# Packed expert weights, blocked activations and a re-cut last norm in a decoder layer with 64 experts

## The chip, the cores and the metric

The kernel runs on one core of one Trainium2 chip. The metric is the device time of one launch in microseconds (us); runs of a kernel are compared by their median. A profile is one execution of its own: its span is counted from the first instruction to the last, and its own time lies a little above its span.

A core has five engines with a program each: TensorE (PE, with its weight load shown apart as PEld), VectorE (DVE), ScalarE (ACT), GpSimd (POOL) and SyncE (SP). They meet through semaphores. SP, ACT and POOL issue the DMAs, which 16 DMA engines carry out.

## The reference, cut to what matters

One decoder layer in f32 on 32 batches of 256 tokens with 256 features. `_layernorm` comes after each part:

```python
x = _layernorm(x + attn(x))            # 16 heads, rotary positions
x = _layernorm(x + xattn(x, ctx))      # 120 context rows; two softmaxes per head,
                                       # weights a1 - lam * a2
x = _layernorm(x + ffn(x))
# ffn: 64 experts, the best 6 per token
scores = sigmoid(x @ router_weight.T)
top_idx = top_k(scores + expert_bias, 6)
probs = top_scores / (sum(top_scores) + 1e-20)
xs = rows of x, per expert, in 96 slots
y = gelu(xs @ w1[e]) @ w2[e]           # w1: 256x128, w2: 128x256
out[token] += y * probs
shared = gelu(x @ sw1.T) @ sw2.T       # 512 wide, for every token
```

## The kernel before, in words

**Order of the work.** Each engine is wrapped in a class `InOrder` (lines 163 to 188) that makes its instructions keep the order in which the program names them. All instructions are therefore recorded at line 172, and the profile tells them apart only by their tiles. What the kernel decides by hand is this one order per engine.

**Stage one** takes the 32 batches through both attentions and the routing. `Batch.steps` (lines 388 to 483) is a hand-written plan of entries (tick, part, function). A batch begins 16 ticks after the one before it, so several are under way together. In each tick the loop runs the part "pre", then the scores of up to two groups of heads with their row maxima (`maxima`, read by DVE into pad_mx) or their exponentials (`weights`, made by ACT into pt), then the parts "av" and "mm", and "post". Late in a batch's plan, at ticks 59 to 61, `xweigh` on DVE takes the products of the second attention (tr), a reciprocal and the coefficients into `parts`, and POOL subtracts the two into `at`. At ticks 73 to 81 `route` chooses the six experts on DVE (step 2 removes the maxima found so far, and counts the tokens of each expert). `dispatch` then sends each token's row with an indirect DMA from POOL into its slot of `slots`: x, its 64 weights and its number, 1284 bytes. `store` (line 964) writes three things through SP: the transposed activations `x2T_d`, and the starting values of the two arrays `acc`: x in the first, zero in the second.

**The shared feed-forward** is a generator `shared` (lines 204 to 275), cut into pieces and threaded between other work. It goes by 16 blocks of 512 tokens. For each block `load` brings x2T from `x2T_d` through SP, two pieces on PE make h (ACT's gelu turns it into gT), and two pieces one block later make the output, which ACT copies to `y`. Each piece is followed by its ACT operation only when the next piece begins. Two banks of PSUM hold h.

**Stage two** (lines 1010 to 1230) runs the experts by pairs, 32 of them, one pair per turn of its loop ("slot"). A pair goes through four steps, one slot apart: `turn` (PE transposes the expert's rows xs; DVE copies them to xsT), `up` (PE), `gelu` (ACT, hT), `down` (PE), and `scatter`: DVE weighs the two results into `ye` (six buffers), and POOL issues two indirect DMAs that add the 96 rows of each expert into `acc[0]` and `acc[1]`. There are 64 such scatters. Experts are loaded by groups of four: `rows_of` brings xs, `expert_weights` w1t and w2t, with three groups loaded ahead; from then on a group is fetched whenever two pairs are through `down`, 13 fetches, of which the first (at 1703 us) lies before the first scatter and 12 lie among the scatters. All the loads are issued by SP. In two of three slots one piece of the shared feed-forward is run too; from the slot END on, two in each slot.

**The last norm** begins at END. A class `Last` has one object per block of 512 tokens: `fetch` (SP loads both sums from acc), `add` (POOL adds them), `stats` (DVE adds y, takes mean and variance in mv), `scale` (POOL makes rs = variance + eps, rstd = rs to the power of -1/2, and off = -mean * rstd), and `put` (ACT scales and shifts into `o`, SP issues the store). A loop runs add of one block, stats and scale of the one before, and put of the one before that. The tile pool `four` with 10 buffers of 4 KB per partition serves w1t, w2t, the sums a and the outputs o.

Of the kernel before, what the change touches and what calls it, by code (L numbers as in the profile page):

```python
# [36 lines left out]
def tile_decoder_layer(  # L37
# [15 lines left out]
    lams: list,  # L53
    router_wT: bass.AP,
    expert_b: bass.AP,
    w1: bass.AP,
    w2: bass.AP,
    sw1T: bass.AP,
    sw2T: bass.AP,
    out: bass.AP,  # L60
# [3 lines left out]
    S = condT.shape[2]  # L64
    NI = T // P
    NT = B * T
    assert T == 2 * P and S <= P

    const = ctx.enter_context(tc.tile_pool(name="const", bufs=1))
# [3 lines left out]

    slots = dram.tile([NE * CAP, XPW], F32, name="slots")
    acc = [dram.tile([NT + CAP, D], F32, name=f"acc{n}") for n in range(2)]
    x2T_d = dram.tile([D, NT], F32, name="x2T_d")

    ident = const.tile([P, P], F32, name="ident")
    make_identity(nc, ident)
# [117 lines left out]
        return trp.tile([P, 512], F32, tag="tr", name="tr")  # L197


    TB = min(512, NT)  # L200
    NQ = TB // P
    NBLK = NT // TB
    ys, whole = {}, set()
# [1 line left out]
    def shared(ypool):  # L205


        def load(k):
            t = ffn.tile([P, D // P, TB], F32, tag="x2T", name="x2T", bufs=3)
            sp.dma_start(  # L210
                out=t,
                in_=x2T_d[:, k * TB : (k + 1) * TB].rearrange("(c p) t -> p c t", p=P),
            )
            return t

        def gelu(hp, gT):

            act.activation(
                gT.rearrange("p f (q t) -> p f t q", q=NQ),
                hp[:, :, :TB].rearrange("p f (t q) -> p f t q", q=NQ),  # L220
                AF.Gelu_apprx_tanh,
            )

        def keep(k, q2, ps):
            if q2 == 0:
                ys[k] = ypool().tile([P, NQ, D], F32, tag="y", name="y")
            act.copy(ys[k][:, 2 * q2 : 2 * q2 + 2, :], ps)
            if 2 * q2 + 2 == NQ:
                whole.add(k)

        before = None
        loaded = {k: load(k) for k in range(2)}
        gTs = {}
        for k in range(NBLK + 1):
            for f2 in range(2):
                if k == NBLK:
                    continue
                if f2 == 0 and k + 2 < NBLK:
                    loaded[k + 2] = load(k + 2)
                if before:  # L240
                    before()
                hp = scp.tile([P, 2, 512], F32, tag="sc", name="h")
                for f in range(2):
                    f0 = (2 * f2 + f) * P
                    for c in range(D // P):
                        pe.matmul(
                            hp[:, f, :TB],
                            lhsT=w_s1[:, c, f0 : f0 + P],
                            rhs=loaded[k][:, c, :],
                            start=(c == 0),  # L250
                            stop=(c == D // P - 1),
                        )
                gT = gTs[k, f2] = ffn.tile([P, 2, TB], F32, tag="gT", name="gT", bufs=4)
                before = lambda hp=hp, gT=gT: gelu(hp, gT)
                yield
            for q2 in range(NQ // 2):
                if k == 0:
                    continue
                if before:
                    before()  # L260
                ps = bank().rearrange("p (q d) -> p q d", q=2)
                for q in range(2):
                    for f in range(SF // P):
                        pe.matmul(
                            ps[:, q, :],
                            lhsT=gTs[k - 1, f // 2][
                                :, f % 2, (2 * q2 + q) * P : (2 * q2 + q + 1) * P
                            ],
                            rhs=w_s2[:, f, :],
                            start=(f == 0),  # L270
                            stop=(f == SF // P - 1),
                        )
                before = lambda k=k, q2=q2, ps=ps: keep(k - 1, q2, ps)
                yield
        before()
        yield
# [5 lines left out]
    with ExitStack() as one:  # L282
# [101 lines left out]
        class Batch:  # L384
# [13 lines left out]
            def steps(self):  # L398
# [64 lines left out]
                    (60, "mm", self.xback, 0),  # L463
                    (61, "pre", self.xweigh, 0),
                    (61, "mm", self.xback, 1),
                    (62, "pre", self.xweigh, 1),
                    (64, "mm", self.transpose, "bT", lambda: self.at),
                    (65, "pre", self.moved, "bT"),
                    (65, "mm", self.project, "bT", "o", w_xout),
# [7 lines left out]
                    (73, "pre", self.sigmoid),  # L477
                    (73, "post", self.route, 0),
                    (75, "post", self.route, 1),
                    (77, "post", self.route, 2),  # L480
                    (79, "post", self.route, 3),
                    (80, "post", self.route, 4),
                    (81, "mm", self.places),
# [480 lines left out]
            def store(self):  # L964

                cols = slice(self.b * T, (self.b + 1) * T)
                sp.dma_start(
                    out=x2T_d[:, cols].rearrange("(c p) t -> p c t", p=P), in_=self.t["x2T"]
                )
                sp.dma_start(  # L970
                    out=acc[0][cols, :].rearrange("(i p) d -> p i d", p=P),
                    in_=self.xpt[:, :, :D],
                )
                sp.dma_start(
                    out=acc[1][cols, :].rearrange("(i p) d -> p i d", p=P),
                    in_=zero[:, :D].unsqueeze(1).to_broadcast([P, NI, D]),
                )
# [33 lines left out]
    with ExitStack() as two:  # L1011
# [1 line left out]
        four = two.enter_context(tc.tile_pool(name="four", bufs=10))  # L1013
        wk = two.enter_context(tc.tile_pool(name="wk2", bufs=2))
        small = two.enter_context(tc.tile_pool(name="small2", bufs=3))
        ypool = two.enter_context(tc.tile_pool(name="ypool", bufs=NBLK))
        ypools.append(ypool)
        EG = 4
        START = 7
# [20 lines left out]
            dve.tensor_add(idx, token, empty)  # L1040
            return idx

        def expert_weights(eg):
            es = slice(eg * EG, (eg + 1) * EG)
            w1t = four.tile([P, EG, D // P, F], F32, tag="four", name="w1t")
            sp.dma_start(out=w1t, in_=w1[es].rearrange("e (c p) f -> p e c f", p=P))
            w2t = four.tile([P, EG, D], F32, tag="four", name="w2t")
            sp.dma_start(out=w2t, in_=w2[es].rearrange("e p d -> p e d"))
            return w1t, w2t

        class Pair:


            def __init__(self, n):
                self.es = (2 * n, 2 * n + 1)

            def turn(self):
# [13 lines left out]
            def up(self):  # L1071
                self.ps = bank()[:, : 2 * CAP].rearrange("p (e t) -> p e t", e=2)
                for k, e in enumerate(self.es):
                    for c in range(D // P):
                        pe.matmul(
                            self.ps[:, k, :],
                            lhsT=weights_of[e // EG][0][:, e % EG, c, :],
                            rhs=self.xsT[:, k, c, :],
                            start=(c == 0),
                            stop=(c == D // P - 1),  # L1080
                        )
# [5 lines left out]
            def down(self):  # L1087
                self.ps = bank()[:CAP].rearrange("p (e d) -> p e d", e=2)
                for k, e in enumerate(self.es):
                    pe.matmul(  # L1090
                        self.ps[:, k, :],
                        lhsT=self.hT[:, k, :],
                        rhs=weights_of[e // EG][1][:, e % EG, :],
                        start=True,
                        stop=True,
                    )
# [24 lines left out]
        class Last:  # L1121
# [16 lines left out]
            def stats(self):  # L1138
# [4 lines left out]
                for q in range(NQ):  # L1143
                    dve.bn_stats(st[:, q, :], y[:, q, :])
                    dve.bn_aggr(mv[:, q, :], st[:, q, :])

            def scale(self):
                rs = small.tile([P, NQ], F32, tag="rs", name="rs")
                pool.tensor_scalar(rs, self.mv[:, :, 1], LN_EPS, None, ALU.add)
                self.rstd = small.tile([P, NQ], F32, tag="rstd", name="rstd")  # L1150
                pool.tensor_tensor(self.rstd, rs, mhalf[:, :NQ], ALU.pow)
                self.off = small.tile([P, NQ], F32, tag="off", name="off")
                pool.tensor_tensor(self.off, self.mv[:, :, 0], self.rstd, ALU.mult)
                pool.tensor_scalar(self.off, self.off, -1.0, None, ALU.mult)

            def put(self):
                o = four.tile([P, NQ, D], F32, tag="four", name="o")
                for q in range(NQ):
# [4 lines left out]
                        scale=self.rstd[:, q : q + 1],  # L1163
                        bias=self.off[:, q : q + 1],
                    )
                sp.dma_start(
                    out=flat[self.rows, :].rearrange("(p q) d -> p q d", q=NQ), in_=o
                )

# [1 line left out]
        pairs = [Pair(n) for n in range(NP)]  # L1171
        xs_of, idx_of, weights_of = {}, {}, {}
        last = [Last(k) for k in range(NBLK)]
        END = START + NP + 3
        slot = steps = 0
        more = True

        def pieces_on(n):
            nonlocal more
            for _ in range(n):  # L1180
                if more:
                    more = next(pieces, "end") != "end"

        def fetch_for(eg):
            if eg < NE // EG:
                xs_of[eg] = rows_of(eg)
                weights_of[eg] = expert_weights(eg)

        while more or steps < NBLK + 3:
            n = slot - START  # L1190
# [6 lines left out]
                pairs[n - 3].scatter()  # L1197
            if slot == 1:
                for eg in range(3):
                    weights_of[eg] = expert_weights(eg)  # L1200
            if slot == START - 2:
                for eg in range(3):
                    xs_of[eg] = rows_of(eg)
# [7 lines left out]
                pieces_on(2)  # L1211
            if slot >= END and (steps == 0 or steps > NBLK or steps - 1 in whole):
                for part, behind in (
                    (Last.add, 0),
                    (Last.stats, 1),
                    (Last.scale, 1),
                    (Last.put, 2),
                ):
                    if part is Last.add:
                        for k in range(0 if steps == 0 else steps + 2, min(steps + 3, NBLK)):  # L1220
# [15 lines left out]
def _rotary(seq):  # L1236
# [3 lines left out]
    ).astype(np.float32)  # L1240
    angles = (np.arange(seq, dtype=np.float32)[:, None] * freqs[None, :]).astype(np.float64)
    return [np.repeat(f(angles).astype(np.float32), 2, axis=1) for f in (np.cos, np.sin)]


# [45 lines left out]
```

## Time and profile before

| | us |
|---|---|
| median of 3 runs | 1999.38 (1996.08 to 2007.22) |
| the profiled execution's own time | 2002.98 |
| its span | 2001.2 |
| PE busy | 1903.4 (95%) |
| DVE, POOL, ACT busy | 1244.2, 1185.4, 1013.0 |
| PE's mean granted clock | 0.978 of full |

Attention and routing fill the span to about 1650 us, then come the last dispatches (the last is done at about 1700), the experts (to about 1900) and the last norm. In the table of the profile by stage each row gives the stretch, its length, busy time and number of instructions of PE, PEld, DVE, ACT and POOL, the granted clock, the mean busy share of the DMA engines and what they moved. A line of the waits is: the waiting engine and the tile it goes on to write, what it waited for, the total in us, how often, the longest. A line of the timeline is: start, duration, engine, operation with output and inputs and their shapes, how many in a row, and in brackets the idle time before it with what ended it. A DMA line gives the size of each DMA in KB and the median time from issue to landing.

### The profile page before, as it was taken

What the parts mean: (1) busy time and instruction counts of PE and PEld (TensorE: products, weight loads), DVE (VectorE), ACT (ScalarE), POOL (GpSimd) and SP (SyncE); (2) the same over time, 40 slices, a digit from 0 to 9 for tenths busy, and PEclk for the clock granted to TensorE, in tenths of its full rate; (3) what the DMA queues carried; (4) which work ended last, traced back from release to release, by engine and by line L of the source; (5) the groups of instructions that cost most, each with busy time, mean ns of one, the idle gap of its engine ahead of it and who ended that gap; (6) DMA issues with size and microseconds to landing.
All of it is one profiled execution on the core that took longest, in us unless ns stands there. A gap on an engine that the chain in (4) does not pass through costs nothing.

```text
span 2001.2 us, 43322 instructions
## 1 busy us (share of the span) xinstructions
PE 1903.4 (95%) x17800; PEld 1298.4 (65%) x17800; DVE 1244.2 (62%) x2750; ACT 1013.0 (51%) x1445; POOL 1185.4 (59%) x1191
## 2 busy tenths in 40 slices
PE   6999999999999999999999999999999988998977
PEld 3566666666666666666666666666666655766745
DVE  3366777777777777777777777777776643232155
ACT  1445555555555555555555555555555442321356
POOL 6233466666666666666666666666664455244687
PEclk8899999999999999999999999999999979998989
DMA  9100121111111111111111111111100023787495
GB/s 250 47 14 9 34 74 59 49 43 35 36 34 32 34 34 35 33 34 32 32 37 31 32 31 33 32 31 31 32 20 20 18 64 101 193 205 178 65 328 210
DMA packets 131813, 132.06 MB, mean 66 GB/s; under 512 B 32763, under 2 KB 118996, under 8 KB 131616
## 3 DMA queue, kind: packets, MB, share of 16 engines
q1 hardware_dynamic: 103408, 115.22, 18.9%
q0 software_dynamic: 25600, 13.02, 3.9%
q8 instruction: 140, 2.29, 0.5%
q10 hardware_dynamic: 2608, 1.07, 0.3%
q14 instruction: 57, 0.47, 0.1%
HBM read 74.62 MB, written 111.04 MB: 93 GB/s over the span
## 4 chain that ended last, share of the span: by engine, by line
PE 80%; DVE 8%; DMA 6%; POOL 3%; issue 2%; ACT 1%; DVEq 0%; POOLq 0%; SPq 0%; ACTq 0%
PE tr L172 39%; PE sc L172 26%; PE av L172 12%; DMA acc<-ye,idx 5%; PE h L172 3%; DVE pad_mx L172 2%; DVE parts L172 1%; POOL slots L172 1%; ACT pt L172 1%; DVE rd L172 1%; DVE rest L172 1%; DVE count L172 1%; DVE ye L172 1%; DVE sel L172 0%; DMA a<-acc 0%
## 5 line engine op out<-in xcount | busy, mean ns | idle before, releaser
L172 DVE TENSOR_REDUCE pad_mx<-sc 128x4 f32<-128x1024 f32 (+1 forms) x512 | 608.3, 1189 | 373.7 <-PE sc L172 367.3
L172 ACT ACTIVATE pt<-sc 128x1024 f32<-128x1024 f32 (+1 forms) x512 | 523.6, 1025 | 399.6 <-PE sc L172 399.3
L172 PE MATMUL sc<-qT,kT 32*128 32x256 f32 (+1 forms) x4096 | 574.0, 405 | 12.3 <-ACT pt L172 7.8
L172 PE MATMUL sc<-kT,qT 32*128 32x256 f32 (+1 forms) x4096 | 562.1, 394 | 10.5 <-ACT pt L172 5.3
L172 POOL DMA_INDIRECT slots<-xpt,slot x384 | 388.9, 1013 | 95.5 <-issue 91.0
L172 PEld LDWEIGHTS sc<-qT,kT 32*128 32x128 f32 (+1 forms) x4096 | 340.2, 183 | 127.7 <-issue 66.0
L172 PEld LDWEIGHTS sc<-kT,qT 32*128 32x128 f32 x4096 | 347.5, 184 | 93.2 <-DVE pad_mx L172 24.5
L172 POOL TENSOR_TENSOR qT<-qT,mT 128x512 f32<-128x512 f32 x128 | 163.5, 1296 | 144.9 <-ACT mT L172 144.9
L172 PE MATMUL tr<-w_qkv,xT 128*128 128x256 f32 (+1 forms) x512 | 193.0, 511 | 8.6 <-DMA xT<-in_xT 8.6
L172 POOL TENSOR_SCALAR rs<-mv 128x2 f32<-128x2 f32 (+1 forms) x80 | 31.0, 388 | 241.9 <-DVE mv L172 240.6
L172 POOL DMA_INDIRECT acc<-ye,idx x64 | 90.1, 1408 | 108.5 <-DVE ye L172 54.4
L172 ACT COPY ot<-av 128x512 f32<-128x512 f32 x192 | 112.3, 585 | 78.5 <-PE av L172 78.4
L172 PEld LDWEIGHTS tr<-w_qkv,xT 128*128 128x128 f32 x512 | 90.6, 191 | 77.7 <-issue 72.4
L172 PE MATMUL av<-pt,pad_v 128*32 128x256 f32 x2048 | 125.3, 385 | 10.2 <-DVE parts L172 10.2
L172 PE MATMUL h<-x2T,w_s 128*128 128x512 f32 x256 | 116.1, 603 | 13.7 <-DMA a<-acc 12.0
L172 PE MATMUL av<-pt,pad_xv 120*32 120x256 f32 x2048 | 126.8, 388 | 0.1
L172 POOL TENSOR_TENSOR rc<-qkb,cosr 128x512 f32<-128x512 f32 x64 | 82.5, 1289 | 71.7 <-DVE qkb L172 66.6
L172 PE MATMUL tr<-w_s,gT 128*128 128x256 f32 x512 | 117.2, 387 | 1.1 <-DVE ye L172 1.1
L172 ACT COPY kT<-tr 128x512 f32<-128x512 f32 (+1 forms) x128 | 70.3, 574 | 89.3 <-PE tr L172 89.3
L172 PEld LDWEIGHTS tr<-w_s,gT 128*128 128x128 f32 x512 | 99.5, 195 | 19.3 <-issue 3.8
L172 POOL TENSOR_TENSOR at<-parts 128x256 f32<-128x256 f32 x64 | 46.4, 725 | 107.3 <-DVE parts L172 107.3
L172 POOL TENSOR_TENSOR pad_qk<-rc,qkb 128x256 f32<-128x256 f32 x128 | 104.9, 841 | 5.0
(141 smaller groups left out, 2844.3 us busy)
## 6 DMA issues: line engine op xcount, KB each, us to landing
a<-acc SPq DMA_DIRECT2D x32, 512.0 KB, 5.6
xT<-in_xT SPq DMA_DIRECT2D x32, 256.0 KB, 6.5
xt<-in_x SPq DMA_DIRECT2D x32, 256.0 KB, 2.8
x2T_d<-T SPq DMA_DIRECT2D x32, 256.0 KB, 2.2
acc<-xpt SPq DMA_DIRECT2D x32, 256.0 KB, 2.7
acc<-zero SPq DMA_DIRECT2D x32, 256.0 KB, 3.0
x2T<-x2T_d SPq DMA_DIRECT2D x16, 512.0 KB, 7.8
w1t<-in_w SPq DMA_DIRECT2D x16, 512.0 KB, 6.8
```

Of the source, the lines that this page charges most:

```text
L172: ins = f(*args, **kwargs)
```

## The change

It has five parts.

1. The experts' weights are packed on the host, one array per pair of experts: for each of 128 partitions, and each expert of the pair, the two halves of w1 and then w2, 512 values. A pair's load is one DMA of 128 rows of 4 KB, 32 loads in all. Before, w1t came in rows of 512 B and w2t in rows of 1 KB, 16 loads each, for groups of four experts. The bytes are the same, and so are PE's instructions.
2. `x2T_d` is laid out by blocks of 512 tokens, so that a block's load has 128 rows of 4 KB where it had 256 of 2 KB. The stores keep pieces of 1 KB. The loads have four buffers and run three blocks ahead, issued in the second h piece of a block.
3. `xweigh` of the second half moves from the start of tick 62 to the end of tick 61, and step 2 of `route` from the end of tick 77 to the start of tick 78. Tick 61 of one batch is tick 77 of the one before it, so the two swap places on DVE.
4. In the last norm DVE makes rs and off; POOL keeps only the power. `put`'s store is issued by ACT. Per step the order is offset, put, add, stats, scale.
5. The pool of y has 14 buffers, was 16; END is one slot later; the slot in between (its n is 35, and 35 % 3 is 2) has neither a pair nor a piece.

The diff, cut:

```diff
-    x2T_d = dram.tile([D, NT], F32, name="x2T_d")
+    x2T_d = dram.tile([NT // TB, P, D // P, TB], F32, name="x2T_d")
...
-            t = ffn.tile([P, D // P, TB], F32, tag="x2T", name="x2T", bufs=3)
-            sp.dma_start(
-                out=t,
-                in_=x2T_d[:, k * TB : (k + 1) * TB].rearrange("(c p) t -> p c t", p=P),
-            )
+            t = ffn.tile([P, D // P, TB], F32, tag="x2T", name="x2T", bufs=4)
+            sp.dma_start(out=t, in_=x2T_d[k])
...
-        loaded = {k: load(k) for k in range(2)}
+        loaded = {k: load(k) for k in range(3)}
...
-                if f2 == 0 and k + 2 < NBLK:
-                    loaded[k + 2] = load(k + 2)
+                if f2 == 1 and k + 3 < NBLK:
+                    loaded[k + 3] = load(k + 3)
...
-                    (62, "pre", self.xweigh, 1),
+                    (61, "post", self.xweigh, 1),
...
-                    (77, "post", self.route, 2),
+                    (78, "pre", self.route, 2),
...
-                sp.dma_start(
-                    out=x2T_d[:, cols].rearrange("(c p) t -> p c t", p=P), in_=self.t["x2T"]
-                )
+                k, t0 = divmod(self.b * T, TB)
+                sp.dma_start(out=x2T_d[k, :, :, t0 : t0 + T], in_=self.t["x2T"])
...
-        ypool = two.enter_context(tc.tile_pool(name="ypool", bufs=NBLK))
+        ypool = two.enter_context(tc.tile_pool(name="ypool", bufs=NBLK - 2))
...
-            w1t = four.tile([P, EG, D // P, F], F32, tag="four", name="w1t")
-            sp.dma_start(out=w1t, in_=w1[es].rearrange("e (c p) f -> p e c f", p=P))
-            w2t = four.tile([P, EG, D], F32, tag="four", name="w2t")
-            sp.dma_start(out=w2t, in_=w2[es].rearrange("e p d -> p e d"))
-            return w1t, w2t
+            wt = four.tile([P, 2, D // P * F + D], F32, tag="four", name="wt")
+            sp.dma_start(out=wt, in_=w12[n])
+            return wt
...
+                self.rs = small.tile([P, NQ], F32, tag="rs", name="rs")
+                dve.tensor_scalar(self.rs, mv[:, :, 1], LN_EPS, None, ALU.add)
...
-                pool.tensor_scalar(rs, self.mv[:, :, 1], LN_EPS, None, ALU.add)
...
-                pool.tensor_tensor(self.off, self.mv[:, :, 0], self.rstd, ALU.mult)
-                pool.tensor_scalar(self.off, self.off, -1.0, None, ALU.mult)
+                dve.scalar_tensor_tensor(
+                    self.off, self.mv[:, :, 0], -1.0, self.rstd, ALU.mult, ALU.mult
+                )
...
-                sp.dma_start(
+                act.dma_start(
                     out=flat[self.rows, :].rearrange("(p q) d -> p q d", q=NQ), in_=o
                 )
...
-        END = START + NP + 3
+        END = START + NP + 4
...
+        def weights_for(eg):
+            for n in range(eg * EG // 2, (eg + 1) * EG // 2):
+                weights_of[n] = expert_weights(n)
...
                 for part, behind in (
+                    (Last.offset, 2),
+                    (Last.put, 2),
                     (Last.add, 0),
                     (Last.stats, 1),
                     (Last.scale, 1),
-                    (Last.put, 2),
```

More of the change, by code (lines that the diff above doesn't have):

```diff
@@ L55, in tile_decoder_layer @@
     expert_b: bass.AP,
-    w1: bass.AP,
-    w2: bass.AP,
+    w12: bass.AP,
     sw1T: bass.AP,
@@ L66, in tile_decoder_layer @@
     NT = B * T
+    TB = min(512, NT)
     assert T == 2 * P and S <= P
@@ L197, in bank @@
         return trp.tile([P, 512], F32, tag="tr", name="tr")
-    TB = min(512, NT)
     NQ = TB // P
@@ L1041, in tokens_of, with expert_weights @@
             return idx
-        def expert_weights(eg):
-            es = slice(eg * EG, (eg + 1) * EG)
-            w1t = four.tile([P, EG, D // P, F], F32, tag="four", name="w1t")
-            sp.dma_start(out=w1t, in_=w1[es].rearrange("e (c p) f -> p e c f", p=P))
-            w2t = four.tile([P, EG, D], F32, tag="four", name="w2t")
-            sp.dma_start(out=w2t, in_=w2[es].rearrange("e p d -> p e d"))
-            return w1t, w2t
+        def expert_weights(n):
+            wt = four.tile([P, 2, D // P * F + D], F32, tag="four", name="wt")
+            sp.dma_start(out=wt, in_=w12[n])
+            return wt
         class Pair:
             def __init__(self, n):
+                self.n = n
                 self.es = (2 * n, 2 * n + 1)
@@ L1076, in up @@
                             self.ps[:, k, :],
-                            lhsT=weights_of[e // EG][0][:, e % EG, c, :],
+                            lhsT=weights_of[self.n][:, k, c * F : (c + 1) * F],
                             rhs=self.xsT[:, k, c, :],
@@ L1092, in down @@
                         lhsT=self.hT[:, k, :],
-                        rhs=weights_of[e // EG][1][:, e % EG, :],
+                        rhs=weights_of[self.n][:, k, D // P * F :],
                         start=True,
@@ L1145, in stats, with offset @@
                     dve.bn_aggr(mv[:, q, :], st[:, q, :])
+                self.rs = small.tile([P, NQ], F32, tag="rs", name="rs")
+                dve.tensor_scalar(self.rs, mv[:, :, 1], LN_EPS, None, ALU.add)
             def scale(self):
-                rs = small.tile([P, NQ], F32, tag="rs", name="rs")
-                pool.tensor_scalar(rs, self.mv[:, :, 1], LN_EPS, None, ALU.add)
                 self.rstd = small.tile([P, NQ], F32, tag="rstd", name="rstd")
-                pool.tensor_tensor(self.rstd, rs, mhalf[:, :NQ], ALU.pow)
+                pool.tensor_tensor(self.rstd, self.rs, mhalf[:, :NQ], ALU.pow)
+            def offset(self):
                 self.off = small.tile([P, NQ], F32, tag="off", name="off")
-                pool.tensor_tensor(self.off, self.mv[:, :, 0], self.rstd, ALU.mult)
-                pool.tensor_scalar(self.off, self.off, -1.0, None, ALU.mult)
+                dve.scalar_tensor_tensor(
+                    self.off, self.mv[:, :, 0], -1.0, self.rstd, ALU.mult, ALU.mult
+                )
             def put(self):
@@ L1186, in fetch_for @@
                 xs_of[eg] = rows_of(eg)
-                weights_of[eg] = expert_weights(eg)
+                weights_for(eg)
         while more or steps < NBLK + 3:
@@ L1199, in tile_decoder_layer @@
                 for eg in range(3):
-                    weights_of[eg] = expert_weights(eg)
+                    weights_for(eg)
             if slot == START - 2:
@@ L1242, in _rotary, with _pairs_of_experts @@
     return [np.repeat(f(angles).astype(np.float32), 2, axis=1) for f in (np.cos, np.sin)]
+def _pairs_of_experts(w1, w2):
+    up = w1.reshape(NE, D // P, P, F).transpose(0, 2, 1, 3).reshape(NE, P, D // P * F)
+    both = np.concatenate([up, w2], axis=2)
+    return both.reshape(NE // 2, 2, P, -1).transpose(0, 2, 1, 3)
 def kernel(**inputs):
@@ L1270 @@
         "expert_b": a["L0_ffn_expert_bias"],
-        "w1": a["L0_ffn_w1"],
-        "w2": a["L0_ffn_w2"],
+        "w12": _pairs_of_experts(a["L0_ffn_w1"], a["L0_ffn_w2"]),
         "sw1T": a["L0_ffn_sw1"].T,
```

## The prediction, made before the result was known

> **What bounds the kernel now.** I read the page first, then the windows by stage, the waits, the DMA view of the expert stage, and the timeline where a wait ends.
>
> ```profile
> PE 1903.4 (95%) x17800; PEld 1298.4 (65%) x17800; DVE 1244.2 (62%) x2750; ACT 1013.0 (51%) x1445; POOL 1185.4 (59%) x1191
> ...
> PE 80%; DVE 8%; DMA 6%; POOL 3%; issue 2%; ACT 1%; DVEq 0%; POOLq 0%; SPq 0%; ACTq 0%
> ```
>
> The matmul engine carries the chain. The windows (us, then busy and count for PE, PEld, DVE, ACT, POOL, then clock, DMA share, GB/s) show where it does not:
>
> ```profile
> 160.00:1500.00 1340.00, 1329.42 (x14158) 907.18 (x14158) 964.40 (x2069) 763.10 (x1098) 844.51 (x858) 1.00 0.12 35
> ...
> 1750.00:1800.00 50.00, 47.14 (x256) 35.41 (x254) 15.67 (x45) 12.36 (x19) 20.76 (x15) 1.00 0.89 213
> 1800.00:1850.00 50.00, 41.99 (x192) 31.18 (x193) 13.49 (x41) 8.13 (x14) 23.26 (x18) 0.90 0.77 177
> ...
> 1900.00:1950.00 50.00, 38.01 (x122) 23.57 (x121) 26.69 (x73) 26.37 (x37) 40.81 (x38) 0.86 0.92 333
> ```
>
> The attention loop leaves PE 10.6 us idle in 1340. The expert stage has DMA at 0.77 to 0.89, and PE begins to stall in it. The waits (us, times, longest) say for what:
>
> ```profile
> DVE ye L172 <- DMA acc<-ye,idx: 63.2, 16, 8.1
> ```
>
> The 64 scatters add rows into two arrays. Their landing frees the six ye buffers, and PE waits behind DVE. The DMA view while weights load (1720 to 1780), and its scatter row after the loads end (1850 to 1900; last column us to landing):
>
> ```profile
> w1t<-in_w SPq DMA_DIRECT2D x7, 512.0 KB, 7.2
> w2t<-in_w SPq DMA_DIRECT2D x7, 512.0 KB, 6.8
> xs<-slots SPq DMA_DIRECT2D x7, 481.5 KB, 4.6
> x2T<-x2T_d SPq DMA_DIRECT2D x2, 512.0 KB, 10.1
> acc<-ye,idx POOLq DMA_INDIRECT x19, 6.5
> ```
> ```profile
> acc<-ye,idx POOLq DMA_INDIRECT x23, 3.3
> ```
>
> A load burst costs a scatter 3.2 us. From the timeline: scatter 1 is issued at 1719.60, the last at 1897.38, landing about 1902.4; four scatters (one burst) take 11.4 to 14 us while loads run, 8.2 us after. The excess is about 3.75 us per burst (12 fetches of a group lie among the scatters), 45 us. PE alone needs 4.37 us per pair, 140 us for 32 pairs, so some 28 us at most could be won there before PE binds. The timeline of PE's stall at its longest, and of the stage of the last norm (start, us, engine, operation, then idle time before it and who ended it):
>
> ```profile
> 1834.37 2.02 PE L172 MATMUL tr<-w2t,hT 128*96 128x256 f32 x4 [4.89 <-DVE ye L172]
> ...
> 1912.17 1.22 POOL L172 TENSOR_SCALAR rs<-mv 128x4 f32<-128x4 f32 x1
> ...
> 1924.52 9.42 PE L172 MATMUL h<-x2T,w_s 128*128 128x512 f32 x16 [11.99 <-DMA a<-acc]
> ...
> 1989.59 7.97 ACT L172 ACTIVATE o<-y,off,rstd 128x256 f32<-128x256 f32 x16
> ```
>
> PE stops at 1912.5 and resumes at 1924.52, because a gelu on ACT stands behind two puts that wait for the sum of the scattered rows. The time of the end follows the last scatter's landing one to one (PE resumes 22 us after it), then PE runs to 1989, and ACT makes four puts.
>
> **Packed weights.** 32 loads of 512 KB stay 32 loads of 512 KB; the rows change from 512 B and 1 KB to 4 KB. In the trace's packets a 512 B row takes 34 to 37 ns, a 1 KB row 47 to 51, a 1284 B row of xs 79 to 82, a 2 KB row 84 to 105 and a 4 KB row (a, out) 159 to 180. Per DMA engine (of 16) a burst is now xs 24 x 0.080 = 1.9 us, w1t 64 x 0.035 = 2.2, w2t 32 x 0.049 = 1.6: 5.7 us. After it is 1.9 + 2 x 8 x 0.170 = 4.6: 1.1 us less. Times 12 is 13 us of DMA time, not on any path unless a scatter waits for it. One end is therefore -12 us. For the other end I ask what stands ahead of a scatter. The rows that went ahead of the delayed ones count 78 to 91 per engine, or about 55 KB: the 24 of xs and most of the 64 of w1t (up to 4.1 us), while w2t comes behind. With 4 KB rows there are 24 + 16, and the nearest row is scatter 63, which met one a load in 4 KB rows: 7 of the 8 rows per engine went first (1.6 us). So all that has arrived goes first: 1.9 + 2.7 = 4.6, +0.5 us for the first scatter of a burst; the second one, which stood behind the whole 5.7, gets 1.1 us back. The two scatters feed two arrays whose chains run side by side, each waiting for its own last landing, with POOL issuing both in order; the later one sets the pace. Between +0.6 and -1.0 per burst I take the middle, -0.2: 12 x -0.2 = **-2 us**; ends -12 and +7.
>
> [...]
>
> **Activations by blocks.** 16 loads of 256 x 2 KB become 128 x 4 KB: 16 x 0.09 = 1.4 us per engine now, 8 x 0.17 = 1.4 after: nothing. Three loads go ahead instead of two, half a step earlier, in a fourth buffer; PE waits for no x2T, so nothing is won. On SP the first three and then a fourth load come before the last batches' stores; those stores (0.36 us issue) wait behind them for at most one issue each. In 4 to 5 bursts an x2T load meets a scatter, 1.4 us in which 2 KB rows could be overtaken and 4 KB rows, by scatter 63, cannot. I take 0; up to +7 (5 x 1.4).
>
> **Weighing before the choice.** A pure swap on DVE: six operations of 1107.82 to 1109.56 (1.74 us) go ahead of the top-6 selection (1106.69 to 1107.8, 1.1 us). The parts come 1.1 us sooner, POOL's at too, and "PE av <- DVE parts" (10.2 us in 27 batches, 0.35 in the batch I followed) may go. But the next thing PE waits for is the reduction behind both, 1109.56 to 1110.71 (PEld sc waits 0.41 for it), and DVE has no gap from 1099.66: it ends where it did. So the stall moves to the scores 1.9 us later. I take 0; ends -9.5 (all of it) and +2 (the dispatch, whose slots come later by 1.7 us once).
>
> **Last norm.** On POOL, rs (1.22 to 1.27 us beside a DVE add; 0.23 in the tail where DVE is idle), and two small ones (0.20 + 0.25) leave for DVE as two operations of 128x4; DVE's 0.1 to 0.2 us rows of that size price them at 0.3 together. For the first block 1.25 + 0.45 - 0.3 is about 1.25 us, in line with put, gelu and PE's resumption: **-1.25 us**. In the later blocks POOL's cycle of 5.39 us hides beneath PE's 6.9 us per slot, and stays hidden; the new one (DVE statistics 3.45, rs, pow 1.04 on POOL, off, semaphores: about 5.1) hides as well. DVE's off now waits for POOL's pow with the next block's statistics behind it; cover 6.9 - 5.1 = 1.8 us.
>
> The 16 out stores move from SP to ACT. Issues on ACT in the trace's start take 0.34 to 0.49 us, and ACT first waits for its own writes. In the stream this hides (ACT is busy 31.28 of 52 us), but behind it stand gelus for which PE's h bank waits: put 2.08 + two gelus 3.7 + 0.6 = 6.4 of 6.9 us. In the tail it doesn't: after the last copy ACT makes four puts in 7.97 us without a gap, and three issues now lie between them, 3 x (0.4 + 0.15) = **+1.65 us**; ends 0 and +3. SP's fetches no longer queue behind a store: nothing, since DMA (0.92) and PE bind there. The y buffers, two fewer, and END, one slot later in which no piece falls, change no order on PE: nothing.
>
> Sum: 0 - 2 + 0 - 1.25 + 1.65 = -1.6. Against the profiled execution's own 2002.98 (span 2001.2) that is 2001.4; the median of the runs is 3.6 lower, 1999.38, so I say 1998 for the likeliest case.
>
> **Rivals.** (1) The bursts' work is the price: the later scatter binds, and each burst gives 1.0 us back: -12 - 1.25 + 1.65 = -11.6, 1988. For it: DMA is near full (0.89), so less work must show somewhere; against: landings wait for what is ahead, not for the mean. A further end, no scatter delay at all, would be -28, 1971. (2) Slower: long rows shut the scatters out. The first scatter of a burst binds, +0.5 in 7 bursts and 0.5 + 1.4 in 5 with an x2T load: 3.5 + 9.5 = +13, 2012; it is slower than a measurement can tell from about +0.85 us a burst. For it: scatter 63; against: w2t's rows no longer follow. (3) The swap doesn't do what it says, or all: 0 or -9.5.
>
> **Numbers.** Likeliest case (within some 8 us of 1998) 0.44; rival 1 0.28, with its far end 0.04 of that; rival 2 0.24; rival 3's gain 0.04. The range takes in rivals 1 and 2, 1984 to 2014. A measurement tells about 0.5%, 10 us: faster 0.30, same 0.45, slower 0.25.
>
> **What would show it.** Right: packets of wt near 170 ns; scatter landing near 6.5 us still while loads run; last scatter issued near 1895; first put 1.25 us sooner after the first sum; ACT's tail near 9.5 us instead of 7.97; PE's idle in the attention loop unchanged. Rival 1: landing below 5.5 and "DVE ye <- DMA acc" down by some 15 us. Rival 2: landing above 7.5, and that wait up. I am wrong above all if a scatter's place among rows of 4 KB isn't what one scatter showed.

## The result and the profile after

The changed kernel takes 2074.01 us (median of 6 runs, 2070.12 to 2077.33), the kernel before 2002.33 on the same occasion: 1.0359 times the time, 95% interval 1.0336 to 1.0383, 72 us slower. The forecast was 1998, 1984 to 2014. The page and the windows after:

```profile
PE 1918.6 (92%) x17800; PEld 1302.5 (63%) x17800; DVE 1312.9 (63%) x2782; ACT 1014.4 (49%) x1445; POOL 1161.1 (56%) x1143
...
PE 72%; DVE 15%; DMA 5%; POOL 4%; issue 3%; ACT 1%; POOLq 0%; SPq 0%; DVEq 0%; ACTq 0%
```
```profile
160.00:1500.00 1340.00, 1295.27 (x13728) 878.57 (x13728) 967.50 (x1997) 738.53 (x1063) 820.20 (x832) 0.99 0.12 35
1950.00:2000.00 50.00, 35.23 (x109) 21.25 (x108) 32.57 (x65) 21.05 (x30) 22.29 (x13) 0.83 0.85 300
2000.00:2076.00 76.00, 43.61 (x165) 30.89 (x163) 54.98 (x111) 38.40 (x58) 31.13 (x20) 0.82 0.44 157
```

DVE's share of the chain has doubled, from 8% to 15%, and its busy time has grown by 69 us, though POOL only gave it 32 tiny operations. PE is idle for 45 us in the attention loop, 10.6 before, and the last stretch has DVE and not PE as its busiest engine. The places, from the start of the first scatter and of the last one in both profiles:

| stretch, us | before | after | difference |
|---|---|---|---|
| start to first scatter | 1719.60 | 1769.07 | +49.5 |
| first to last scatter | 177.8 | 179.2 | +1.4 |
| last scatter to the end | 103.8 | 126.9 | +23.1 |
| span | 2001.2 | 2075.2 | +74.0 |

The loads, the change's largest part, moved next to nothing. Two small parts did nearly all of it: the swap on DVE, and the last norm's small operations that went from POOL to DVE. First the attention loop. In the timeline of before, the operations that the swap touches:

```profile
1107.21 0.29 DVE L172 TENSOR_TENSOR sel<-vals,rest 128x128 f32<-128x128 f32 x1
1107.42 0.48 DVE L172 TENSOR_TENSOR count<-count,sel 128x64 f32<-128x64 f32 x2
...
1109.56 1.15 DVE L172 TENSOR_REDUCE pad_mx<-sc 128x8 f32<-128x960 f32 x1
...
1109.74 0.73 POOL L172 TENSOR_TENSOR at<-parts 128x256 f32<-128x256 f32 x1 [2.31 <-DVE parts L172]
1110.43 1.26 POOL L172 TENSOR_TENSOR xt<-xt,b_out 128x512 f32<-128x512 f32 x1
```

And the same operations in the timeline after:

```profile
1142.40 0.72 POOL L172 TENSOR_TENSOR at<-parts 128x256 f32<-128x256 f32 x1 [1.17 <-DVE parts L172]
...
1142.75 0.53 DVE L172 TENSOR_TENSOR sel<-vals,rest 128x128 f32<-128x128 f32 x1
1143.10 1.33 POOL L172 TENSOR_TENSOR xt<-xt,b_out 128x512 f32<-128x512 f32 x1
1143.20 1.63 DVE L172 TENSOR_TENSOR count<-count,sel 128x64 f32<-128x64 f32 x2
...
1144.76 1.14 DVE L172 TENSOR_REDUCE pad_mx<-sc 128x8 f32<-128x960 f32 x1
...
1145.96 0.47 PE L172 MATMUL sc<-kT,qT 32*128 32x240 f32 x2 [1.67 <-DVE pad_mx L172]
```

Before, POOL's subtraction and bias addition (they follow the weighing) ran beside DVE's reduction, which kept its 1.15 us. After the swap they run beside the selection and the counting. They end only when POOL's operation is over: the selection at 1143.28, the subtraction at 1143.12; the first of the two countings, 1.30 us long, at 1144.50, the addition at 1144.43. They take 0.53 + 1.63 us where they took 0.29 + 0.48, the reduction is that much later, and PE waits 1.67 us for it in every batch.

Then the last norm. Timeline after, two blocks and the end:

```profile
1964.67 2.33 POOL L172 TENSOR_TENSOR a<-a,a 128x1024 f32<-128x1024 f32 x1
1964.71 2.31 DVE L172 SCALAR_TENSOR_TENSOR off<-mv,rstd 128x4 f32<-128x4 f32 x1 [1.15 <-POOL rstd L172]
1966.94 1.21 DVE L172 TENSOR_TENSOR y<-y,a 128x1024 f32<-128x1024 f32 x1
1967.06 2.08 ACT L172 ACTIVATE o<-y,off,rstd 128x256 f32<-128x256 f32 x4 [21.91 <-DVE off L172]
...
1971.74 2.30 DVE L172 SCALAR_TENSOR_TENSOR off<-mv,rstd 128x4 f32<-128x4 f32 x1 [1.13 <-POOL rstd L172]
...
1978.55 9.76 PE L172 MATMUL h<-x2T,w_s 128*128 128x512 f32 x16 [14.77 <-ACT gT L172]
...
2069.22 0.16 DVE L172 SCALAR_TENSOR_TENSOR off<-mv,rstd 128x4 f32<-128x4 f32 x1 [1.21 <-POOL rstd L172]
```

off on 4 columns takes 2.31 us while POOL adds the sums, and 0.16 us at the end, when POOL has nothing to add. As off stands ahead of the next block's statistics on DVE, a block now takes 7.0 to 7.1 us. Before, POOL's additions of neighbouring blocks came 5.38 us apart:

```profile
1925.87 2.35 POOL L172 TENSOR_TENSOR a<-a,a 128x1024 f32<-128x1024 f32 x1
...
1931.25 2.35 POOL L172 TENSOR_TENSOR a<-a,a 128x1024 f32<-128x1024 f32 x1
```

From the first put to the last there are 102.4 us (1967.06 to 2069.42), and there were 80.3 (1915.17 to 1995.5): 22.1 us more. The end no longer follows PE, which is through at 2043.6, 31.6 us before the end; before, it was 12.2.

### The profile page after: what moved, and what is told of

The parts are those of the page before. It is cut to its first block, busy times and chain, and to the rows that moved or that the text cites. A ratio compares the mean times of both kernels' runs of the same rounds, so it can differ in the third digit from the quotient of the medians.

```text
span 2075.2 us, 43268 instructions
## 1 busy us (share of the span) xinstructions
PE 1918.6 (92%) x17800; PEld 1302.5 (63%) x17800; DVE 1312.9 (63%) x2782; ACT 1014.4 (49%) x1445; POOL 1161.1 (56%) x1143
## 4 chain that ended last, share of the span: by engine, by line
PE 72%; DVE 15%; DMA 5%; POOL 4%; issue 3%; ACT 1%; POOLq 0%; SPq 0%; DVEq 0%; ACTq 0%
PE tr L172 36%; PE sc L172 25%; PE av L172 9%; DMA acc<-ye,idx 4%; DVE pad_mx L172 4%; DVE count L172 2%; PE h L172 2%; DVE parts L172 1%; DVE off L172 1%; DVE rd L172 1%; DVE st L172 1%; POOL slots L172 1%; POOL rstd L172 1%; DVE sel L172 1%; ACT pt L172 1%
## 5 line engine op out<-in xcount | busy, mean ns | idle before, releaser
L172 POOL TENSOR_SCALAR rs<-mv 128x2 f32<-128x2 f32 x64 | 14.0, 218 | 237.8 <-DVE mv L172 237.8
L172 PE MATMUL tr<-ident,ot 128*128 128x128 f32 x768 | 103.3, 277 | 0.2 <-ACT ot L172 0.2
```

Source lines behind the costliest of these rows:

```text
L172: ins = f(*args, **kwargs)
```

## The experiments

The theory after this reading: a DVE operation on two tensors of SBUF (in this kernel the tiles outside PSUM and DRAM) waits until POOL's running tensor operation is over. The rivals: the new order itself makes the chains longer (route behind the weighing; one handover more between POOL and DVE per block); the stores on ACT cost the end; and, for the loads, what the forecast left open. Three chips were used: e1 to e4 ran on one, where the kernel before takes 2004.76 us, e5 to e8 on a second (2004.59 us), and e9 to e12 on a third, where it takes 2055.48 us and a batch 49.4 in the three kernels that leave it alone (e9 to e11). Each ratio is to the kernel before on the same chip.

**Undoing the parts.** e1 undoes the swap, e2 the last norm's move to DVE, e3 all but the loads and the two sizes.

```diff
# e1, from the changed kernel
-                    (61, "post", self.xweigh, 1),
+                    (62, "pre", self.xweigh, 1),
...
-                    (78, "pre", self.route, 2),
+                    (77, "post", self.route, 2),
# e2, from the changed kernel
-                self.rs = small.tile([P, NQ], F32, tag="rs", name="rs")
-                dve.tensor_scalar(self.rs, mv[:, :, 1], LN_EPS, None, ALU.add)
...
-                dve.scalar_tensor_tensor(
-                    self.off, self.mv[:, :, 0], -1.0, self.rstd, ALU.mult, ALU.mult
-                )
+                pool.tensor_tensor(self.off, self.mv[:, :, 0], self.rstd, ALU.mult)
+                pool.tensor_scalar(self.off, self.off, -1.0, None, ALU.mult)
```

> The changed kernel with the weighing and the choice back in their old places, all else as changed. The changed kernel spends 49.5 us more before its first scatter. If the swap alone makes them (selection and counting now run on DVE while POOL subtracts and adds, 0.53 + 1.63 us instead of 0.29 + 0.48), some 46 us go and the time is near 2028, with the counting back at 0.23 us and PE's wait for pad_mx back below 1 us a batch. If the blocked activations or their earlier loads do it, the time stays near 2074.

> The changed kernel with rs and off back on POOL and the old order of a step; ACT still issues the stores. If off on DVE is what costs (2.30 us beside POOL's add, a step of 7.1 us against PE's 6.9), the stage from the last scatter to the end goes from 126.9 to about 106 and the time to about 2053. If the stores on ACT cost it, it stays near 127.

> The kernel before with the packed weights, the blocked activations and the sizes of two pools only. By the forecast's step for the expert stage: -2 us, so 2000, no difference that can be told. If 13 us less of DMA work were passed on: 1988. If the long rows shut the scatters out: 2012.

e1: 1.0135 (1.0105 to 1.0165), so the swap is 2.24% or 45 us; the counting is back at 0.231 us, a batch at 48.81. e2: 1.0247 (1.0209 to 1.0284), so rs and off on DVE, with the new order of a step, are 1.12% or 22 us; last scatter to end is 106.3 us. e3: 1.0014 (1.0000 to 1.0029). The parts add up: 2.24 + 1.12 + 0.14 = 3.50 of 3.59%.

**The bias addition moved away (e5).** The swapped order stays; only POOL's 1.33 us operation leaves the place.

```diff
-                    (-2, "pre", self.bias_x),
+                    (2, "pre", self.bias_x),
```

> The changed kernel with one edit: POOL adds the bias to x (xt<-xt,b_out, 1.33 us, which runs beside DVE's counting) four ticks later, where POOL idles. The order on DVE stays that of the change. If DVE's two-input operations wait out POOL's tensor operation, the counting goes from 0.81 back to 0.23 us (2 x 0.57 per batch), the selection keeps its 0.53 (the subtraction still runs beside it), and 30 to 45 us go: near 2035. If the swapped order itself makes the chain longer, the time stays near 2074.

1.0156 (1.0130 to 1.0182): 2.03% or 41 us back. The groups of DVE in e5 (last columns: busy, mean ns of one):

```profile
L172 DVE TENSOR_TENSOR sel<-vals,rest 128x128 f32<-128x128 f32 x32 | 16.6, 519 | 1.1
L172 DVE TENSOR_TENSOR count<-count,sel 128x64 f32<-128x64 f32 x63 | 14.6, 232 | 1.1
```

The counting, no longer beside POOL's addition, costs what it did before; the selection, still beside POOL's subtraction, keeps its 519 ns. A batch takes 48.98 us, against 50.15 in the changed kernel and 48.82 before: the 0.17 left is the selection's excess. The order costs little; what runs beside it costs the most.

**The sign back on POOL (e4).** One handover more per block, but POOL's addition can't start while DVE makes off.

```diff
-                dve.scalar_tensor_tensor(
-                    self.off, self.mv[:, :, 0], -1.0, self.rstd, ALU.mult, ALU.mult
-                )
+                dve.tensor_mul(self.off, self.mv[:, :, 0], self.rstd)
+                pool.tensor_scalar(self.off, self.off, -1.0, None, ALU.mult)
```

> The changed kernel, but DVE only multiplies mean and rstd, and POOL turns the sign before its next add, so that this add can't start while DVE makes off. That is one more handover from DVE to POOL per block. If off's 2.30 us are POOL's add being waited out, off falls to about 0.2 us, a step gets shorter than PE's 6.9 us and some 15 to 20 us go: about 2056. If it is the chain between the two engines, each block gets about 0.3 us longer: about 2079.

1.0258 (1.0225 to 1.0291), 1.0% or 20 us back; last scatter to end 105.7 us. Timeline of e4:

```profile
1994.84 0.16 DVE L172 TENSOR_TENSOR off<-mv,rstd 128x4 f32<-128x4 f32 x1 [1.23 <-POOL rstd L172]
1994.91 1.22 DVE L172 TENSOR_TENSOR y<-y,a 128x1024 f32<-128x1024 f32 x1
1995.09 1.13 POOL L172 TENSOR_SCALAR off<-off 128x4 f32<-128x4 f32 x1 [0.29 <-DVE off L172]
...
1996.19 2.36 POOL L172 TENSOR_TENSOR a<-a,a 128x1024 f32<-128x1024 f32 x1
```

off takes 0.16 us again and a block 5.0. The third line is the mirror image: now POOL's tiny operation waits out DVE's addition, 1.13 us, as rs did before the change (1.22). With one step more in the chain the time is less, so the longer chain was not the cause.

**A plain delay on DVE (e12).** To see what any lengthening at this place costs, the order of before with an unrelated one-input operation ahead of the reduction.

```diff
                 pool.tensor_sub(self.at[:, i, :], parts[:, 0, :], parts[:, 1, :])
+                if i == 1:
+                    dve.reciprocal(idle_o, idle_i)
```

> The kernel before, its order kept, with one reciprocal of 184 elements (some 1.4 us, one input, result unused) put on DVE once per batch behind the weighing, ahead of the reduction. [...] If the swap's price is DVE's added time ahead of that reduction and nothing else about the swap, this costs about the same: PE waits about 1.7 us per batch, a batch takes 50.1 to 50.3 us instead of 48.82, and the dips of the clock (five batches of 51.8 us in the changed kernel, one of 49.7 before) come with it: about 2046. If the dips belong to the collision, they don't come: about 2038.

1.0150 (1.0132 to 1.0168). The operation took 1.29 us, no more than expected, with POOL's subtraction and addition beside it, PE waited 1.03 us for pad_mx, and a batch took 50.51 us where its neighbours on that chip took 49.4. So DVE has next to no cover there: 1.29 us of it cost 1.1. The dips of the clock that the expectation speaks of did not come, though PE idles for 45.6 us in the loop, as long as in the changed kernel (44.7): the single gaps are shorter (see the last section).

**The swap on its own merit (e6), and a version of my own (e8, e11).** e6 is before with the swap and the later bias. e8 is e6 with rs on DVE and put one step later (`(Last.put, 3)` for 2). e11 is before with put two steps later (4 for 2, rstd and off in four buffers, one turn of the loop more), all else untouched.

```diff
# e8, beside the edits of e6
+                self.rs = small.tile([P, NQ], F32, tag="rs", name="rs")
+                dve.tensor_scalar(self.rs, mv[:, :, 1], LN_EPS, None, ALU.add)
...
-                    (Last.put, 2),
+                    (Last.put, 3),
# e11, from the kernel before
-                    (Last.put, 2),
+                    (Last.put, 4),
```

> The kernel before with the swap and with the bias addition four ticks later, nothing else of the change. If the swap costs only through the shared access, its own merit shows: PE's wait for parts (10.2 us) goes, its wait for pad_mx grows by the 0.22 us of the selection per batch (some 6 us): 1990 to 2000 where before has about 2003. If the order itself costs, some 45 us more: 2048.

> e6 and two more edits on the last norm: rs (variance + eps) is made by DVE at the end of its statistics, and a block's put comes one step later, so that ACT's gelus stand ahead of the first put. POOL's cycle per block falls from 5.39 to about 4.3 us and keeps off, so no two-input operation is added to DVE. If PE's 12 us stop at the start of the last norm was only the order on ACT, it shrinks by most of that: about 1985. If the stop is needed by something else (a full bank, the sums), only e6's gain stays, about 1995.

> The kernel before with a block's put two steps later, all else as before, so that ACT's gelus stand ahead of the first puts. PE stopped for 12 us at the start of the last norm before, and for 6.3 us with the put one step later. If only the order on ACT stops it, the stop is gone; then POOL's 16 cycles of 5.39 us, from 1906 on, bind: about -3 us, 2001. If the end follows PE, -10 us: 1994.

e6: 1.0031 (1.0021 to 1.0041), a miss: no gain even without the worst collision. The "shared access" of the expectation is the author's guess at a cause; what the runs show are the durations. PE's wait for parts is gone (0.3 us in all), but its wait for pad_mx has 15.0 us more, 0.52 in nearly every batch, as the reduction is where it was plus the selection's excess. e8: 1.0012 (1.0002 to 1.0021), below e6 by 0.2%, also less than hoped. In its timeline:

```profile
1980.15 2.36 POOL L172 TENSOR_TENSOR a<-a,a 128x1024 f32<-128x1024 f32 x1
...
1980.99 1.54 DVE L172 TENSOR_SCALAR rs<-mv 128x4 f32<-128x4 f32 x1
```

rs has one tensor input, and still it waits for POOL's addition, 1.54 us for 0.17 alone. My theory of two inputs was too narrow, and the block's cycle came down to 5.07 us only, not to 4.3. e11: 0.9986 (0.9975 to 0.9996), -3 us, the only kernel here with all of its loads that is below the kernel before: PE's 12 us stop is gone, and the end follows POOL's cycles of 5.39 us as worked out (PE is through 19.9 us before the end).

**The loads (e9, e10, e7).** e9 is before with the packed weights alone, e10 with the blocks alone. e7 is e3 without every second load of the weights, so that half of the pairs compute with the weights of the pair before:

```diff
-                weights_of[n] = expert_weights(n)
+                weights_of[n] = weights_of[n - 1] if n % 2 else expert_weights(n)
```

> The kernel before with the packed weights alone (and the two sizes of part 5). The stretch from first to last scatter is 177.8, 177.6 and 176.6 us in three kernels with the old loads and 179.2 to 184.1 in five with both new ones. If the packed rows of the weights cost the difference, it is about 182 here; if the blocks of activations do, about 177. The time then is 1.001 to 1.003 or 1.000 of before.

> The kernel before with the blocked activations alone, loaded three blocks ahead. If the blocks cost the 4 us in the expert stage, the stretch from first to last scatter is about 182 us here and about 177 with the packed weights alone; if the weights do, the other way round.

> The kernel e3 (loads only) with every second pair using the weights of the pair before it, so half of the experts' weights are not loaded and those pairs compute with wrong ones. A burst has 1.35 us less of DMA work per engine. If the work of the bursts sets the pace of the scatters, the stretch from first to last scatter (184.1 us in e3, 177.8 before) falls by some 12 to 16 us and the time to about 1990. If what is served ahead of a scatter is limited by bytes (about 55 KB per engine in either layout, xs 30 and most of two loads), it falls by 12 x 0.5 = 6 us at most.

e9: 1.0004 (0.9993 to 1.0015), 178.6 us from first to last scatter. e10: 1.0005 (0.9992 to 1.0019), 179.4 us. Neither shows the 4 us that the profiles on the other two chips suggested (and e11, with the old loads, has 179.8 there), so that difference stays unsettled and small. e7: 0.9958 (0.9935 to 0.9980), 173.9 us, where e3 has 184.1 and the other kernels with both loads 179.2 to 182.5: 5 to 10 us for 16 us of work taken away. The DMA view after, weights loading (1770 to 1830):

```profile
wt<-in_w SPq DMA_DIRECT2D x14, 512.0 KB, 6.2
xs<-slots SPq DMA_DIRECT2D x7, 481.5 KB, 4.9
x2T<-x2T_d SPq DMA_DIRECT2D x3, 512.0 KB
acc<-ye,idx POOLq DMA_INDIRECT x19, 3.7
```

The scatters' median landing fell from 6.5 to 3.7 us in the window, yet their last is no earlier, and DVE's wait for them (ye) fell only from 63.2 to 61.1 us. From the packets of the second pair's scatters: before, 78 and 83 rows per engine went ahead of their first row (54 and 56 KB, 3.2 and 3.4 us late); after, 27 and 14 rows (52 and 57 KB, 2.8 and 3.0 us). In these four cases about the same number of bytes goes ahead, whatever the rows' length, and the scatters win 0.4 us, not 1.1.

## Why the prediction was wrong

- **"Weighing before the choice ... a pure swap on DVE ... it ends where it did. I take 0."** This step failed, by 45 us, beyond its ends of -9.5 and +2. The order of events was right: without the collision with POOL's addition the reduction does end where it did (e5, e6: +0.17 us a batch). What failed is the assumption that DVE's operations keep their durations. I noted that POOL's subtraction comes sooner "too", and didn't ask what would run beside it. Shown by e1 and e5: 0.22 us for the selection and 2 x 0.57 for the counting (means of the loop, 0.53 - 0.30 and 0.81 - 0.23), 1.37 a batch; the batch grew by 1.33. Over the 25 undisturbed batches that is 33 us; dips of the clock (below) add 8.4, and the rest of 49.5 lies in the start (3.5; this varies, as the first store comes between 199 and 207 us in these profiles) and in the first and last batches.
- **"DVE's 0.1 to 0.2 us rows of that size price them at 0.3 together ... hides as well ... cover 6.9 - 5.1 = 1.8 us"; "-1.25 us."** Failed by 22 us, in two terms. The first is the price of off. The rows of that size had no POOL operation beside them; off is issued in the moment that POOL goes from its power to its addition, so it meets it in nearly every block: 2.30 us, not 0.15, and the block takes 5.1 + 2.15 = 7.2, measured 7.1. The second is the cover. Against PE's 6.9 a block of 7.1 would have lost 0.2, some 3 us in all. But PE's pieces of 6.9 us stand beside only some nine of the 16 blocks (PE ran from 1924.5 to 1989 before), and the others have none: the 15 steps from the first put to the last took 80.3 us before, 5.35 each. So POOL's 5.39 did not hide beneath 6.9; it was nearly all that the end allowed (e4, at 5.0 a block, took 82.3 us, no less). After, 13 steps of 7.1 and two of 5.0, with no addition beside off, make the 102.4. The first put came 10.2 us after the first sum began instead of 8.95, and not 1.25 sooner.
- **The row was there.** The forecast quotes POOL's rs at 1.22 us beside a DVE addition and 0.23 with DVE idle. I read it as POOL's weakness, worth taking off POOL, and didn't ask whether DVE's operations lengthen in the same way. The trace of before has that too: in the batch at 715.82 us POOL's subtraction came at 716.14, and selection and countings took 0.58 + 1.07 us, against medians of 0.29 and 2 x 0.225. With these rows both edits could have been questioned beforehand: the swap puts selection and counting beside POOL's subtraction and addition in every batch (0.53 + 1.63 us after), and the last norm puts off beside POOL's sum (2.30 us). How many inputs an operation has doesn't decide it: selection, counting and off have two, and rs in e8, with one, took 1.54 us for 0.17. Why one engine's operation lengthens beside the other's, no run here shows.
- **The packed weights, -2 us (ends -12 and +7).** Inside the ends: +1.4 in the profile, 1.0014 and 1.0004 in e3 and e9. But this is in part luck, as the working was partly wrong: "all that has arrived goes first" would have put 24 + 16 rows ahead, 94 KB per engine; 52 to 57 KB went. Two sums are loose: the +0.6 and -1.0 a burst are 0.1 off their own working (+0.5 and -1.1), and the far end's 28 us doesn't come out, as 177.8 - 140 is 38 and PE idles for only 10.9 of the 177.8 us before. The result hangs on neither.
- **The blocks, 0; the stores on ACT, +1.65.** The first held (e10, 1.0005). For the second, e2's last stretch is 106.3 us and e3's 103.4: 2.9 us, of one profile each, inside the ends of 0 and +3. Of these the three issues in ACT's tail make 1.7, near the forecast: the last puts of e2 come 2.55 us apart, those of e3 1.97. In the profile after, an issue on ACT takes 0.34 us and starts 0.02 us after the last operation of its put ends (2061.55 and 2061.57); the forecast's 0.15 for ACT's wait was the author's estimate, and the two spacings show 0.58 for issue and wait together. In the changed kernel itself ACT no longer sets the end.
- **The rival on the slower side** was the wrong one: long rows before the scatters. None of my rivals had an engine slowed by another's operation.

## What to carry to other kernels

Before moving an operation between or along DVE and POOL, list what the other engine runs in that moment, and look in the trace for the same operation with two durations: the slower one names what it waits for (rs on POOL, 1.26 and 0.23 us in the kernel before). A tiny operation on one of these engines can cost the rest of the other's long one (off: 2.30 us for 0.16), so its price is not its size. Not every operation waits: DVE's reduction of sc took 1.15 us with POOL's addition beside it as well. An operation that is moved also releases its followers at a new moment, and they are part of the change.

## What the runs showed of the hardware that was not expected

In the changed kernel most batches take 50.15 us, but five of the 25 in the middle take 1.64 to 2.63 us more. Windows of one plain batch and the next, after:

```profile
355.40:405.50 50.10, 48.42 (x522) 32.84 (x518) 36.59 (x76) 27.79 (x40) 31.62 (x32) 1.00 0.13 42
405.50:457.20 51.70, 50.02 (x520) 33.93 (x516) 36.48 (x77) 27.79 (x40) 31.53 (x32) 0.97 0.13 40
```

The same work, PE's busy time 1.6 us longer and its granted clock 0.97. In finer windows of the slow batch:

```profile
434.22:437.63 3.41, 1.73 (x26) 1.09 (x19) 2.19 (x4) 0.86 (x3) 2.93 (x4) 1.00 0.01 0
437.63:441.05 3.42, 3.42 (x11) 2.69 (x10) 1.34 (x3) 0.77 (x1) 0.74 (x1) 0.50 0.01 0
441.05:444.46 3.41, 3.41 (x41) 2.72 (x43) 2.29 (x7) 2.50 (x5) 0.09 (x1) 1.00 0.02 5
```

The clock is halved for one stretch of 3.41 us, which loses 1.7 us. Between 160 and 1500 us there are five such stretches in each of the three kernels with a 1.67 us gap of PE in every batch (after, e2, e4), and none in any other kernel here. The five make 8.5 us. Within a kernel their starts lie whole multiples of 3.41 us apart. With all of the time cut at that spacing, each of the 15 halved stretches follows one in which PE was busy for no more than 51% of the time, because the gap lay in it. In e12, with as much idle time in gaps of 1.1 us at most, no stretch is below 57%.

So the dips came only in the kernels with the gaps; but about two in three stretches at 51% were not followed by one. It came when a gap of 1.7 us began 0.09 to 0.41 us into its stretch (13 times), and after two of three longer gaps of 2.4 us; what sets it stays open.
